# Where in a step two edge chunks share one TensorE product: a graph layer on one core

## The chip, the cores and the metric

The kernel runs on one core of a Trainium2 chip. A core has five engines with queues of their own: TensorE (matrix products; in the profile PE for the matmuls and PEld for the weight loads that go with them), VectorE (DVE), ScalarE (ACT), GpSimd (POOL) and SyncE (SP, which here only starts transfers). Sixteen DMA engines move data between HBM and the core's memory. The metric is the device time of one execution in microseconds.

## The reference

One layer of a graph network on 12,500 nodes of 128 numbers and 412,500 edges of 48 numbers, all float32. The edges are sorted by their destination node.

```python
h = jnp.maximum(_layernorm(x, axis=-1), 0.0)
agg = segment_sum(edge_attr_48, dst, num_segments=12500)      # 48 sums per node
u = graph_globals[0]                                           # the same for every node
hid = relu(concatenate([h, agg, u]) @ W1 + b1)                 # 240 -> 256
out = x + hid @ W2 + b2                                        # 256 -> 128
```

## The kernel before

**Chunks and steps.** 896 edges (128 partitions by T = 7) are a chunk. A step `s` takes CS = 8 chunks, 1.4 MB of edges, in two halves `h` of CH = 4 chunks; there are NS = 58 steps, the last one short. A chunk's edges go to a stretch of neighbouring nodes, and a one-hot matrix of W = 32 columns (`oh`, made by VectorE at L294) says which node of its window each edge belongs to.

**The sums of a step** (`aggregate`, from L314) are products of the one-hots (the weights) with the edges (the moving operand), added up in a PSUM tile `ps`. A single product takes one chunk and one value of t: 32 weight columns, 48 moving columns, and writes 32 of the 128 partitions; four of them, one for each chunk of a half, fill the partitions. A paired product takes two chunks at once: 64 weight columns and 96 moving columns. It gives four blocks of sums of which two are wanted; for the second chunk of a pair these lie in columns 48 to 95. One value of t in one half, a row in what follows, is thus four single products or two pairs. `twos[h]` is the number of rows of half `h` that are done in pairs; before the change they come first in the half (`t < twos`). Each product, being float32, leaves four records on TensorE: two weight loads and two matmuls.

**After the sums**, `keep_sums` (from L335, on ScalarE) copies `ps` to `sums`, with small copies of the odd chunks' other columns for the halves that have pairs. Two steps later (one in the last steps) `place` (TensorE, tile `pp`) moves the sums to their nodes and `add` (VectorE) adds them to the running table `aggT`.

**Between the sums** the layer itself runs in pieces, for blocks of 512 nodes: transposes of the normalised nodes (`turn`, tile `pt`), the first layer (`first_h`, `first_a`, tile `ph`), ReLU on ScalarE, the second layer (`second`, tile `po`), the result on VectorE and a store on GpSimd's queue. The order is written out by hand: a planner gives each piece a half-step `k` by a cost in us (`piece`), and the main loop emits for each step: `place`, the pieces of 2s, `add`, the pieces of 2s + 1, the sums, and ScalarE's copies.

**How many pairs.** The planner counts the products of the step, `n`, those since the last step's sums included, and reckons the time of TensorE, `us`, as 1.8 plus the pieces' costs. As long as `us` is below 0.08 us for each product, one more row is done in pairs, in the second and the first half by turns; a row adds 0.08 us to `us` and takes two from `n`. In the first steps `spare` products (a product of constants, L593 on, whose result nobody reads) are emitted at half-steps 1, 3, 5, 7 and 9.

**Loads.** SyncE issues the edges as 230 loads of two chunks, four to a step, three steps ahead. A load waits for the fifth load before it to land (`few`, at most 5 in flight) and for the TensorE product that was emitted last when the load was emitted. There are 18 buffers of two chunks.

At the end a flag tells whether the edges' order allowed all this; with these inputs the general path behind it (from L816 on) is not run.

Of the kernel before, what the change touches and what calls it, by code (L numbers as in the profile page):

```python
# [22 lines left out]
def kernel(  # L23
# [26 lines left out]
    T = 7  # L50
# [9 lines left out]
    NSF = NCH // CS  # L60
    TAIL = E - NCH * CE
    NS = NSF + 1
# [78 lines left out]
    with fast:  # L141
# [34 lines left out]
        def product(*a, **k):  # L176
            count[0] += 1
            last[:] = [nc.tensor.matmul(*a, **k).ins.name]  # L178
# [100 lines left out]
        def load(s, i):  # L279
            if s >= NS or s == NSF and i > 1:  # L280
                if s == NSF and i == 2:
                    edges[s].append(etail)
                return
            for c in (2 * i,):
                e = ep.tile([P, 2, T * DE], F32, name="e")
                few(load_edges(e, s * CS + c, 2))
                edges.setdefault(s, []).extend([e[:, 0], e[:, 1]])
                both.setdefault(s, []).append(e)

        def onehot(s):  # L290
            oh = ohp.tile([P, CH, T, 2, W], F32, name="oh")

            def compare(to, n, r):
                nc.vector.tensor_tensor(  # L294
                    to, iota[:, None, :W].to_broadcast([P, n, W]), r[:, :, None].to_broadcast([P, n, W]), OP.is_equal)

            def chunks(a, b):
                compare(oh[:, a // 2:b // 2].rearrange("p c t u w -> p (c t u) w"), (b - a) * T,
                        rel[:, (s * CS + a) // 2:(s * CS + b) // 2].rearrange("p c t u -> p (c t u)"))

            if s == NSF:
                chunks(0, CH)
                compare(oh[:, CH // 2, :TT, 0], TT, relt[:, :TT])
            elif s < 2:
                chunks(0, CH)
                chunks(CH, CS)
            else:
                chunks(0, CS)
            onehots[s] = oh
# [4 lines left out]
        def aggregate(s, h, twos):  # L314
            left = s == NSF and h
            if h == 0:
                banks_s[s] = ps_agg.tile([P, 512], F32, name="ps")[:, :4 * DE].rearrange("p (h f) -> p h f", h=2)
            ps, es, oh = banks_s[s], edges[s], onehots[s]
            n = TT if left else T
            for t in range(n):  # L320
                first, end = t == 0 and h == 0, t == n - 1
                if t < twos:
                    for q in range(0, CH, 2):
                        c = CH * h + q
                        product(ps[W * q:W * (q + 2), h], oh[:, c // 2, t], both[s][c // 2][:, :, t * DE:(t + 1) * DE],
                                start=first, stop=end, skip_group_check=True)
                    continue
                for q in range(1 if left else CH):
                    c = CH * h + q
                    o = DE * (q % 2) if twos else 0  # L330
                    product(
                        ps[W * q:W * (q + 1), h, o:o + DE], oh[:, c // 2, t, c % 2], es[c][:, t * DE:(t + 1) * DE],
                        start=first, stop=end, skip_group_check=True)

        def keep_sums(s, twos):  # L335
            ps = banks_s.pop(s)
            to = sums[s % NSB].rearrange("p h (u f) -> p h u f", u=2)[:, :, :, :DE]

            def keep_these(k, h, o):
                nc.scalar.copy(to[k, h], ps[k, h, None, o:o + DE].to_broadcast(  # L340
                    [k.stop - k.start, h.stop - h.start, 2, DE]))

            if s < NSF:
                keep_these(slice(0, P), slice(0, 2), 0)
            else:
                keep_these(slice(0, P), slice(0, 1), 0)
                keep_these(slice(0, W), slice(1, 2), 0)
            hs = [h for h in range(2) if twos[h]]
            for q in range(1, CH, 2) if hs else ():
                keep_these(slice(W * q, W * (q + 1)), slice(hs[0], hs[-1] + 1), DE)  # L350

        def place_columns(s):
            po = ohp.tile([P, 2, WP], F32, name="place")
            nc.vector.tensor_tensor(po, iota[:, None, :WP].to_broadcast([P, 2, WP]),  # L354
                                    pos[:, s, :, None].to_broadcast([P, 2, WP]), OP.is_equal)
            places[s] = po

        def place(s):
            banks_p[s] = pp = ps_p.tile([P, 512], F32, name="pp")
            po = places.pop(s)  # L360
            for h in range(2):
                k = W if s == NSF and h else P
                product(pp[:HI + DE, SECOND * h:SECOND * h + WP], sums[s % NSB][:k, h, :HI + DE], po[:k, h],
                                 start=(h == 0), stop=(h == 1), skip_group_check=True)

        def add(s):
            _, v = nc.values_load_multi_w_load_instructions(
                at_i[0:1, s:s + 1], engines=[DVE], min_val=low(s), max_val=high(s),
                skip_runtime_bounds_check_because="clamped to these on the chip")
            to = aggT[:, ds(v[0], WG)]  # L370
            nc.vector.tensor_tensor(to, to, banks_p.pop(s)[:HI + DE, :WG], OP.add)  # L371
# [186 lines left out]
        with tc.manual_schedule():  # L558
# [71 lines left out]
            def at(k, f, *a):  # L630
                todo.setdefault(max(0, k), []).append((f, a))


            def placed(s):
                return min(s + 2, max(LATE, s + 1))
# [48 lines left out]
            for j in range(NBL):  # L684
                k = where["turn", j]
# [13 lines left out]
            def apart(k, f, *a):  # L699
                while k - 1 in taken or k in taken or k + 1 in taken:  # L700
                    k -= 1
                taken.add(k)
                at(k, f, *a)
                return k
# [6 lines left out]
            at(6, middles, 1)  # L711
            at(10, check_dst, 0)
            at(12, check_dst, 1)
            for k in range(1, 10, 2):
                at(k, spare)
            for i in range(2, len(parts)):
                need = 2 * (parts[i][0] // CS - (4 if i == len(parts) - 1 else 0))
                k = apart(need - 4, middles, i)
                at(k + 2, check_dst, i)
                k = apart(k - 1, spread_dst, i, 1)  # L720
                k = apart(k - 1, spread_dst, i, 0)
# [5 lines left out]
            k = apart(2 * (NS - 6), verdict)  # L727
# [10 lines left out]
                at(where["turn", j], keep, j)  # L738
            assert placed(ready[x1]) < NS

            ALL, MORE, EACH_US = 1.8, 0.08, 0.08
            counted = count[0]
            for s in range(NS):
                now = [p for p in range(NS) if placed(p) == s]
                paced[:] = [s] * (s > 0)

                def next_load(i):
                    if s > 0:
                        load(s + AHEAD - 1, i)

                if s < LATE:
                    for p in now:
                        place(p)
                next_load(0)
                for f, a in todo.pop(2 * s, []):
                    f(*a)
                next_load(1)
                if s < LATE:
                    for p in now:
                        add(p)  # L760
                for f, a in todo.pop(2 * s + 1, []):
                    f(*a)
                next_load(2)
                if s >= LATE:
                    for p in now:
                        place(p)
                        add(p)


                us = ALL + work.get(2 * s, 0.0) + work.get(2 * s + 1, 0.0)  # L770
                n, twos = count[0] - counted + CS * T, [0, 0]
                for h in (1, 0) * T:
                    if us < EACH_US * n and s < NSF:
                        twos[h] += 1
                        us += MORE
                        n -= 2
                aggregate(s, 0, twos[0])
                aggregate(s, 1, twos[1])
                counted = count[0]
                next_load(3)  # L780
                keep_sums(s, twos)
                if s == 1:
                    place_columns(0)
                if s > 0:
                    place_columns(s)
                if s + EARLY < NS:
                    onehot(s + EARLY)
# [166 lines left out]
```

## Time and profile before

| | |
|---|---|
| time, median of 3 runs | 323.09 us (321.39 to 323.69) |
| the profiled execution | 322.37 us, its span 320.6 us |
| busy: TensorE, VectorE, ScalarE, GpSimd | 309.6, 232.4, 174.7, 77.2 us |
| bytes moved | 95.14 MB, 297 GB/s over the span |
| records on TensorE | 6171 matmuls, 6172 weight loads |
| first sums, last sums | 8.8 us, 305.3 us |

In a row of the timeline, the first number is the start in us from the span's start, the second how long the group lasts, then engine, source line, operation, written tile <- read tiles, the shape, and the number of records; in square brackets stands idle time before it and what ended it. Records of one line and the same tiles are merged, and a merged row shows the shape of its first record only. The shape 128*64 128x96 is a paired product, 128*32 128x48 a single one. Matmuls overlap and their ends are modelled, so a group's length overstates it: the distance from its start to the start of the next group is what it costs. In a row of the windows stand the stretch, its length, the busy time and number of records of each engine, the granted clock of TensorE, the share of the DMA engines and the rate in GB/s. A row of the waits names who waited, what ended it, the sum in us, the number of times and the longest.

### The profile page before, as it was taken

How to read it: one execution, taken by the hardware profiler on the slowest of the kernel's cores; microseconds unless marked ns; L12 is line 12 of the kernel's file. 1: busy time of each engine (PE TensorE's matmuls, PEld its weight loads, DVE VectorE, ACT ScalarE, POOL GpSimd, SP SyncE). 2: the span in 40 equal slices, each digit the busy share in tenths (PEclk: the TensorE clock that was granted, in tenths of full speed). 3: DMA queues.
4: the chain of work that ended last, by engine and by line, in shares of the span. 5: the costliest groups of instructions: out<-in, count | busy, mean ns of one | idle time of the engine just before them, and what ended most of it. 6: DMA issues, size and time to landing. Idle time of an engine off the chain costs nothing. (4 is left out here: it accounts for less than half of the span.)

```text
span 320.6 us, 14355 instructions
## 1 busy us (share of the span) xinstructions
PE 309.6 (97%) x6171; PEld 235.8 (74%) x6172; DVE 232.4 (72%) x530; ACT 174.7 (54%) x434; POOL 77.2 (24%) x87
## 2 busy tenths in 40 slices
PE   7899999999999999999999999999999999999992
PEld 3587767877787877776887886876787877887772
DVE  6786967785786866749966599769874899687221
ACT  2234795375564765555564486655552974565420
POOL 8221042022201444222224203113303034211000
PEclk9999999999999999999999999999999999999999
DMA  7999999999999999999999999999999999884102
GB/s 234 306 341 315 343 346 333 320 337 311 330 353 313 346 353 335 307 340 356 341 349 330 302 309 303 327 342 333 303 328 323 297 305 343 295 267 141 37 0 75
DMA packets 69716, 95.14 MB, mean 297 GB/s; under 512 B 5018, under 2 KB 64611, under 8 KB 69647
## 3 DMA queue, kind: packets, MB, share of 16 engines
q1 hardware_dynamic: 67439, 87.53, 83.5%
q0 software_dynamic: 2208, 6.63, 5.6%
q8 instruction: 50, 0.82, 1.0%
q14 instruction: 19, 0.16, 0.2%
HBM read 87.74 MB, written 6.40 MB: 294 GB/s over the span
## 5 line engine op out<-in xcount | busy, mean ns | idle before, releaser
L178 PEld LDWEIGHTS ps<-e,oh 128*32 128x32 f32 (+1 forms) x5056 | 108.4, 117 | 37.3 <-issue 8.4
L178 PE MATMUL ps<-e,oh 128*32 128x48 f32 (+1 forms) x5056 | 132.8, 221 | 0.7 <-issue 0.7
L294 DVE TENSOR_TENSOR oh<-iota,rel 128x1792 f32<-128x1792 f32 (+1 forms) x60 | 115.9, 1936 | 0.0
L340 ACT COPY sums<-ps 128x192 f32<-128x192 f32 (+1 forms) x173 | 53.6, 310 | 105.9 <-PE ps L178 103.3
L497 POOL DMA_DIRECT2D out_dram<-ot x25 | 13.9, 559 | 221.0 <-DVE ot L489 172.4
L371 DVE TENSOR_TENSOR aggT<-aggT,pp 112x246 f32 x58 | 23.7, 409 | 48.9 <-PE pp L178 41.3
L178 PE MATMUL po<-w,hid 128*128 128x128 f32 (+1 forms) x384 | 47.7, 276 | 1.3 <-ACTq L816 1.3
L411 POOL TENSOR_TENSOR xb<-xt,b_sb 128x512 f32<-128x512 f32 (+2 forms) x26 | 45.3, 1744 | 14.9 <-DMA xt<-in_x_dram 9.1
L178 PE MATMUL ph<-hT,w1h 128*128 128x512 f32 (+2 forms) x100 | 47.5, 578 | 0.3 <-ACT hT L432 0.3
L178 PEld LDWEIGHTS po<-w,hid 128*128 128x128 f32 (+1 forms) x384 | 44.9, 191 | 2.1 <-ACTq L816 1.4
L418 ACT ACTIVATE xn<-xt,sh,sc 128x128 f32<-128x128 f32 (+1 forms) x98 | 40.5, 482 | 1.1 <-DVE sh L405 0.6
L475 ACT ACTIVATE hid<-ph,bias 128x512 f32<-128x512 f32 (+2 forms) x49 | 30.3, 669 | 19.6 <-PE ph L178 18.4
L178 PE MATMUL pp<-place,sums 128*112 128x128 f32 x232 | 39.3, 292 | 0.0
L354 DVE TENSOR_TENSOR place<-iota,pos 128x256 f32<-128x256 f32 x58 | 34.8, 602 | 0.0
L178 PEld LDWEIGHTS pp<-place,sums 128*112 128x112 f32 x232 | 28.8, 176 | 5.1 <-issue 1.0
L178 PE MATMUL ph<-aggT,w1a 48*128 48x256 f32 (+1 forms) x192 | 28.4, 400 | 0.0
L432 ACT COPY hT<-pt 128x512 f32<-128x512 f32 (+2 forms) x26 | 26.6, 1022 | 0.8 <-PE pt L182 0.5
L489 DVE TENSOR_TENSOR ot<-po,xb 128x512 f32<-128x512 f32 (+2 forms) x25 | 16.6, 665 | 14.2 <-PE po L178 12.8
L178 PEld LDWEIGHTS ph<-aggT,w1a 48*128 48x128 f32 x192 | 17.3, 186 | 10.9 <-issue 7.8
L388 DVE BATCH_NORM_STATS2 st<-xt 128x6 f32<-128x128 f32 (+1 forms) x98 | 21.3, 278 | 1.9 <-DMA xt<-in_x_dram 1.9
L178 PEld LDWEIGHTS ph<-hT,w1h 128*128 128x128 f32 x100 | 16.2, 191 | 6.0 <-issue 3.3
L182 PE MATMUL pt<-ident,xn 128*128 128x128 f32 (+1 forms) x98 | 15.9, 282 | 0.2 <-DVE dev L239 0.2
(120 smaller groups left out, 143.3 us busy)
## 6 DMA issues: line engine op xcount, KB each, us to landing
e<-in_edge_attr_dram SPq DMA_DIRECT2D x230, 336.0 KB, 5.0
xt<-in_x_dram SPq DMA_DIRECT2D x23, 256.0 KB, 5.4
out_dram<-ot POOLq DMA_DIRECT2D x23, 256.0 KB, 5.0
di<-in_dst_dram SPq DMA_DIRECT2D x3, 448.0 KB, 6.9
xt<-in_x_dram SPq DMA_DIRECT2D x2, 128.0 KB, 4.5
out_dram<-ot SPq DMA_DIRECT2D x2, 128.0 KB, 2.8
di<-in_dst_dram SPq DMA_DIRECT2D x1, 154.0 KB
w1h<-in_L_gnn_W_dram POOLq DMA_DIRECT2D x1, 128.0 KB, 5.6
```

The costliest lines, as they stand in the source:

```text
L178: last[:] = [nc.tensor.matmul(*a, **k).ins.name]
L182: last[:] = [nc.tensor.transpose(*a, **k).ins.name]
L294: nc.vector.tensor_tensor(to, iota[:, None, :W].to_broadcast([P, n, W]), r[:, :, None].to_broadcast([P, n, W]), OP.is_equal)
L340: nc.scalar.copy(to[k, h], ps[k, h, None, o:o + DE].to_broadcast([k.stop - k.start, h.stop - h.start, 2, DE]))
L354: nc.vector.tensor_tensor(po, iota[:, None, :WP].to_broadcast([P, 2, WP]), pos[:, s, :, None].to_broadcast([P, 2, WP]), OP.is_equal)
L371: nc.vector.tensor_tensor(to, to, banks_p.pop(s)[:HI + DE, :WG], OP.add)
L388: nc.vector.bn_stats(st[:m, q, :], xs[j][:m, q, :])
L411: nc.gpsimd.tensor_tensor(xb[:m, :r], xs[j][:m, :r], b2_sb[:m, None, :].to_broadcast([m, r, D]), OP.add)
L418: nc.scalar.activation(xn[:m, q], xs[j][:m, q], AF.Relu, bias=shift[j][:m, q:q + 1], scale=scale[j][:m, q:q + 1])
L432: nc.scalar.copy(hT[:, :m * r].rearrange("d (p r) -> d r p", r=r), ht[j][:, :m * r].rearrange("d (r p) -> d r p", r=r))
L475: nc.scalar.activation(to, ph, AF.Relu, bias=bias[:, h:h + 1])
L489: nc.vector.tensor_tensor(ot[:m, :r], pos_o[j][:m, :r], xbs[j][:m, :r], OP.add)
```

## The change

Pairs are now put in the second half of a step alone, at its end: the last `twos` values of t. The time reckoned for TensorE starts at 1.75 instead of 1.8, and 0.15 more is asked before another row is paired. A step has 7 paired rows at most, and steps 54 on have none. The spare products at half-steps 5, 7 and 9 are gone. Worked through, 692 pairs become 576 and 1836 single products become 2068.

```diff
@@ aggregate
             for t in range(n):
                 first, end = t == 0 and h == 0, t == n - 1
-                if t < twos:
+                if t >= n - twos:
                     for q in range(0, CH, 2):
@@ spare products
-            for k in range(1, 10, 2):
+            for k in (1, 3):
                 at(k, spare)
@@ main loop
-            ALL, MORE, EACH_US = 1.8, 0.08, 0.08
+            ALL, TURN, MORE, EACH_US = 1.75, 0.15, 0.08, 0.08
...
                 us = ALL + work.get(2 * s, 0.0) + work.get(2 * s + 1, 0.0)
                 n, twos = count[0] - counted + CS * T, [0, 0]
-                for h in (1, 0) * T:
-                    if us < EACH_US * n and s < NSF:
-                        twos[h] += 1
-                        us += MORE
-                        n -= 2
+                while us + TURN < EACH_US * n and twos[1] < T and s < NS - 4:
+                    twos[1] += 1
+                    us += MORE
+                    n -= 2
```

## The prediction

> **What bounds the kernel now.** I read the page first, then TensorE's timeline step by step, then the waits of SyncE's queue, then the transfers.
>
> ```profile
> PE 309.6 (97%) x6171; PEld 235.8 (74%) x6172; DVE 232.4 (72%) x530; ACT 174.7 (54%) x434; POOL 77.2 (24%) x87
> PE   7899999999999999999999999999999999999992
> PEclk9999999999999999999999999999999999999999
> DMA  7999999999999999999999999999999999884102
> q8 instruction: 50, 0.82, 1.0%
> PE ps L178 <- issue: 0.7, 2, 0.5
> ```
>
> TensorE is busy from the first sums to the last, and in the list of waits its only entry inside the sums is 0.7 us of "issue". So TensorE's own work sets the time, and a microsecond taken out of it counts as long as nothing else is late. The transfers are busy in nearly every slice too, so they are the first candidate for "late". The third is the instruction stream itself: 50 packets of 0.82 MB together are 16 KB each, one for about every 250 of the 12,343 TensorE records (each product leaves four: two weight loads, two matmuls).
>
> What do the sums of one step cost? Both forms, and five steps with the start of whatever follows:
>
> ```profile
> L178 PE MATMUL ps<-e,oh 128*64 128x96 f32 x1384 | 81.9, 255 | 0.0
> L178 PE MATMUL ps<-e,oh 128*32 128x48 f32 x3672 | 62.2, 209 | 0.7 <-issue 0.7
> ...
> 15.94 2.53 PE L178 MATMUL ps<-e,oh 128*64 128x96 f32 x56
> 18.40 0.69 PE L178 MATMUL pp<-place,sums 128*112 128x128 f32 x4
> ...
> 114.55 2.00 PE L178 MATMUL ps<-e,oh 128*64 128x96 f32 x104
> 116.47 0.69 PE L178 MATMUL pp<-place,sums 128*112 128x128 f32 x4
> ...
> 206.58 2.16 PE L178 MATMUL ps<-e,oh 128*64 128x96 f32 x96
> 208.67 0.58 PE L178 MATMUL pp<-place,sums 128*112 128x128 f32 x3
> ...
> 150.06 2.32 PE L178 MATMUL ps<-e,oh 128*64 128x96 f32 x88
> 152.30 0.69 PE L178 MATMUL pp<-place,sums 128*112 128x128 f32 x4
> ...
> 301.09 1.77 PE L178 MATMUL ps<-e,oh 128*32 128x48 f32 x108
> 302.79 1.14 PE L178 MATMUL ph<-aggT,w1a 48*128 48x256 f32 x8
> ```
>
> A step has 14 rows (7 values of t in each half); a row is either four single products or two pairs. The merged rows carry the shape of their first product only, so the record count tells the mix: 104 records are 2 pair rows and 12 single rows, 96 are 4 and 10, 88 are 6 and 8, 108 are 1 and 13, and 56 are 14 pair rows. From start to start these take 1.92, 2.09, 2.24, 1.70 and 2.46 us.
>
> - From 2 to 6 pair rows the time grows by 0.32 us: **a pair row costs 0.08 us more than a single row**.
> - All pairs take 2.46. With 6 pair rows that would be 2.46 - 8 x 0.08 = 1.82, but it took 2.24. Such a step has three changes of form inside (pairs, singles | pairs, singles): **0.14 us for each turn**. The 108-record step, with one pair row and two turns, agrees: 2.46 - 13 x 0.08 + 2 x 0.14 = 1.70.
>
> **The change part by part.**
>
> *Turns and rows.* Working the two loops through with the counts of products, the old rule puts pairs in 346 rows with 161 turns (51 steps have three), the new one in 288 rows with 53 turns (one in each step that has pairs). Of that, steps 0 to 4 have 66 rows and 7 turns, then 35 and 5: 31 x 0.08 + 2 x 0.14 = 2.8 us. Steps 5 to 56 have 280 rows and 154 turns, then 253 and 48: 27 x 0.08 + 106 x 0.14 = 2.2 + 14.8 = **17.0 us** less work for TensorE. A new turn stands in the middle of the step, single to pair, as half of the old ones did, so I price it the same.
>
> *Three spare products.* One is worth what lies between its start and that of the sums:
>
> ```profile
> 18.93 1.02 PE L178 MATMUL ph<-iota,ones 128*128 128x512 f32 x2
> 19.89 2.74 PE L178 MATMUL ps<-e,oh 128*64 128x96 f32 x60
> ...
> 24.47 8.23 SPq L127 DMA_DIRECT2D e<-in_edge_attr_dram  x9
> e<-in_edge_attr_dram SPq DMA_DIRECT2D x230, 336.0 KB, 5.0
> 35.48 1.76 PE L178 MATMUL ps<-e,oh 128*64 128x96 f32 x54
> ```
>
> 0.96 us each, 2.9 in all, in steps 2, 3 and 4. But this work, and the 2.8 us of the same steps, lies over the arrival of the data. Counting four edge loads to a step, the seventh of the nine in the SyncE row, issued near 30 us, is the last of step 5. With the median of 5.0 us to landing it is there at 35.0, and step 5's sums start at 35.48 and need it 0.6 us later, in their second half. So of 5.7 us only about **0.5** can reach step 5; the rest becomes waiting for edges.
>
> *Loads for the rest of the run.* The loads have five in flight at most and are held to TensorE's pace.
>
> ```profile
> 137.90 8.51 SPq L127 DMA_DIRECT2D e<-in_edge_attr_dram  x9
> ...
> 286.27 2.32 SPq L127 DMA_DIRECT2D e<-in_edge_attr_dram  x3
> 304.66 0.80 PE L178 MATMUL ps<-e,oh 128*32 128x48 f32 x56
> ...
> SPq L127 <- DMA e<-in_edge_attr_dram: 58.0, 92, 2.0
> SPq L127 <- PE ps L178: 4.5, 9, 1.2
> ...
> SPq L127 <- PE ps L178: 17.5, 13, 2.6
> SPq L127 <- DMA e<-in_edge_attr_dram: 17.4, 32, 1.2
> ...
> 40.00:60.00 20.00, 19.74 (x438) 14.24 (x437) 13.45 (x32) 14.70 (x37) 5.68 (x6) 1.00 1.01 343
> 140.00:160.00 20.00, 19.52 (x432) 15.07 (x421) 15.82 (x38) 10.67 (x27) 3.62 (x5) 1.00 1.04 348
> 240.00:260.00 20.00, 20.00 (x430) 15.50 (x429) 14.35 (x38) 13.14 (x40) 4.83 (x5) 1.00 0.95 309
> ```
>
> The first pair of SyncE waits is from the window 40 to 190 us, the second from 190 to 290. In the first, loads wait for the landing of earlier loads; in the second as much for TensorE. The head start shows the same. At step 5 it is about nothing. The last load of step 27 (third of nine, near 139.7) lands near 144.7 for sums that start at 150.06: 5.4 us. The last of all is issued near 288.2 and lands near 293.2 for sums at 304.66: 11.5 us. So even on the old timetable the loads would let TensorE be some 11 us earlier at the end, and more where the pace held them back (348 GB/s were moved in one window, 309 in a late one). On the way it is tighter: by step 27 TensorE would gain about 22 x 0.31 (two turns a step and some rows) + 0.5 = 7.3, against 5.4 + 0.6 of head start. I take **2.5 us** of waiting for edges after step 5; the ends are 0 (the loads speed up with TensorE's pace) and 10 (they don't).
>
> *The instruction stream.* 116 pairs fewer are 116 products more, less three spares: 452 more records.
>
> ```profile
> 58.08 1.11 PE L178 MATMUL ps<-e,oh 128*32 128x48 f32 x32 [0.26 <-issue]
> 141.69 0.49 PE L178 MATMUL ps<-e,oh 128*32 128x48 f32 x26 [0.48 <-issue]
> ...
> 57.90:141.60 83.70, 83.13 (x1773) 63.93 (x1773) 60.92 (x131) 48.37 (x115) 22.76 (x21) 1.00 1.00 330
> ```
>
> These are the two "issue" waits, each inside a run of singles, with no data to wait for. Between them lie 3546 TensorE records: 14 blocks of 253, the size of a packet with some semaphore instructions in it. I read them as two late packets. The sums run from 8.8 to 305.3 us, so 12,343 / 253 = 48.8 blocks last 296 / 48.8 = 6.1 us each; 12,795 / 253 = 50.6 in 284 would last 5.6. If every boundary comes 0.5 us sooner, the two late ones are late by some 0.9 each, and a few more, now just in time, are late by a few tenths: **3 us more**, an estimate; the ends are 0 and 25 (all 50 late by 0.5).
>
> On this the Trainium skill, "Runtime: NRT & Kernel Launch", section Instruction fetch mechanics, speaks: instructions come in 16 KiB blocks of 256, fetched ahead, and crossing a block is "mostly hidden" because dispatch is slower than the fill. The block size agrees with the rows above, the two stalls do not bear out the hiding; by the rule the term would be 0 and the time 307.7.
>
> *The rest.* ScalarE's small copies after a step now take one half instead of two, and none in steps 54 to 56; ScalarE is at 54% and the result is placed a step later, so nothing. VectorE goes from 72% to about 75% of a shorter span; nothing unless a one-hot comes late. The weights of the layer, the final products and the last store are unchanged. The pairs now stand after the singles, so nothing new waits ahead of the next step's work except the loads of the second half, which are needed as before.
>
> **Sum.** 17.0 + 0.5 - 2.5 - 3.0 = 12.0. The profiled span is 320.6 and that execution took 322.37, so 310.4; the median of the three timed runs, 323.09, is 0.7 above, which gives 311.1. I predict 310.7. A change under about 1%, 3 us, could not be told from none.
>
> **The rivals.**
>
> 1. *All of TensorE's gain.* The loads follow and the packets stay hidden: 17.5 less, 305.6. For it: the head start of 11.5 us. Against: windows at a DMA share of 1.0 already, and two late packets.
> 2. *The transfers take over.* Singles let TensorE ask for edges faster than 340 GB/s. If the first half of the run stays on its old timetable, the gain there is no more than the head start, and a few us come in the second half: 4 to 7 less than the median, about 317. For it: the 58.0 us of waiting for landings. Against: the loads get ahead of TensorE all the same.
> 3. *The instruction stream takes over (slower).* If TensorE is really fed at one block in 6.1 us, cheaper rows give nothing and 452 more records cost 1.8 blocks: 11 us, 334. It decides once most blocks arrive later than they are used up, 5.6 us. Against: only two such waits in some 48 blocks.
> 4. *A cold clock.* The spare products may be there to keep TensorE at speed.
>
> ```profile
> 1.68 2.07 PE L178 MATMUL ph<-iota,ones 128*128 128x512 f32 x2 [1.68 <-POOL iota L565]
> 5.06 3.78 PE L178 MATMUL ph<-iota,ones 128*128 128x512 f32 x4
> 13.20 0.73 PE L182 MATMUL pt<-ident,df 128*128 128x128 f32 x4 [1.16 <-ACT sums L340]
> ```
>
> Early spares take about twice as long as the one at 18.93 (four in 3.78 against two in 1.02), though the granted clock of the page stands at 9 tenths or more throughout. If the waits for edges in steps 2 to 4, 1 to 1.5 us each, bring that state back, some 8 us of work there last twice as long and about 4 us of it are not covered: 314.7. Against: after 1.16 us of idleness at 13.20 four transposes run at full speed. The Trainium skill, "TensorE: Matmul & The Clock Gate", Part 1, has the clock halve after an idle window of about 3.4 us; no wait that I foresee is so long.
> 5. *It does nothing.* If a turn were a wait for the next chunk's edges and not a cost of the change of form, it would stay: only 27 x 0.08, 2 us, eaten by the packets, 322. Against: the same 0.14 at 150 us, where the edges are 5 us ahead.
>
> **How the numbers follow.** Forecast (307 to 314.5) 0.62; all of the gain 0.08; transfers 0.17; cold clock 0.03; nothing 0.05; slower 0.05. The range 305 to 318.5 takes in the first four but for their edges and leaves out 1 to 2 in 10. Faster by over 1% means below 319.9: 0.62 + 0.08 + 0.17 + 0.03 less 0.03 of the slow end of the transfers, 0.87; within 1% 0.07; slower 0.06.
>
> **What the changed profile would show.** A step with 12 pairs takes 1.96 from its first sum to the next operation, one without pairs 1.34. The entry "issue" inside the sums grows from 0.7 to some 3 us. Waits for edges appear on TensorE in steps 1 to 5 and here and there to step 30. Windows from 40 to 280 move near 340 GB/s. I am wrong if the turns stay at the old price in the new place, if "issue" reaches 10 us, or if TensorE waits for edges in most steps.

## The result and the profile after

The changed kernel takes 312.40 us (median of 4 runs, 310.81 to 314.13) beside 322.24 for the kernel before: a ratio of 0.9694, 95% interval 0.9624 to 0.9765. Timed again with five rounds it took 310.15 us beside 321.83: 0.9637 (0.9601 to 0.9673). Here and below a median is that of all executions, while ratios and intervals leave out slow ones, those over 1.5% above the fastest of the same kernel. The forecast was 310.7, 12.0 us less. The profiled execution of the changed kernel took 310.81, its span is 309.1: 11.5 us less than the span before.

First the page and the waits of the changed kernel, where TensorE's own load was to shrink and "issue" to grow:

```profile
PE 291.4 (94%) x6397; PEld 227.5 (74%) x6398; DVE 231.8 (75%) x530; ACT 164.1 (53%) x426; POOL 78.5 (25%) x87
PEclk9997999999999999999999999999999999999999
q8 instruction: 51, 0.84, 1.1%
...
PE ps L178 <- issue: 4.6, 9, 1.0
PEld ps L178 <- DMA e<-in_edge_attr_dram: 4.6, 8, 0.8
PE ps L178 <- DMA e<-in_edge_attr_dram: 2.5, 5, 0.6
```

226 matmuls and as many weight loads more, the 452 records of the forecast. TensorE is busy 18 us less, and inside the sums it waits more: 4.6 us of issue instead of 0.7, and for edges, which it did not wait for before.

The price of the sums, from the timeline of TensorE (start of the sums, start of what follows), for steps with 4, 8, 12 and no pairs:

```profile
111.06 1.71 PE L178 MATMUL ps<-e,oh 128*32 128x48 f32 x104
112.70 0.69 PE L178 MATMUL pp<-place,sums 128*112 128x128 f32 x4
...
199.22 1.87 PE L178 MATMUL ps<-e,oh 128*32 128x48 f32 x96
201.02 0.69 PE L178 MATMUL pp<-place,sums 128*112 128x128 f32 x4
...
150.61 2.03 PE L178 MATMUL ps<-e,oh 128*32 128x48 f32 x88
152.57 0.69 PE L178 MATMUL pp<-place,sums 128*112 128x128 f32 x4
...
290.04 1.40 PE L178 MATMUL ps<-e,oh 128*32 128x48 f32 x112
291.37 1.14 PE L178 MATMUL ph<-aggT,w1a 48*128 48x256 f32 x8
```

1.64, 1.80, 1.96 and 1.33 us, where the first three mixes took 1.92, 2.09 and 2.24 before: 0.28 us less with the same number of pairs, two turns. That is the gain, read off three steps.

Where the run as a whole gained, the starts of the sums of step 5 and of the last step show:

```profile
31.61 1.37 PE L178 MATMUL ps<-e,oh 128*64 128x96 f32 x26 [0.54 <-DMA e<-in_edge_attr_dram]
...
35.75 2.03 PE L178 MATMUL ps<-e,oh 128*32 128x48 f32 x88
...
293.24 0.80 PE L178 MATMUL ps<-e,oh 128*32 128x48 f32 x56
```

Step 5 starts at 35.75 instead of 35.48: the first five steps gained nothing, and step 4 can be seen waiting for edges ahead of its pairs. From step 5 to the last step it is 257.49 us instead of 269.18, 11.69 less. What follows takes 15.9 us in both. So of 17.0 us of work saved, some 5.3 were lost again on the way, to packets, edges or both; the experiments are about that.

SyncE's waits between 190 and 290 us, the two rows that were equal before:

```profile
SPq L127 <- DMA e<-in_edge_attr_dram: 41.4, 64, 2.0
...
SPq L127 <- PE ps L178: 0.8, 3, 0.3
```

The pace of TensorE holds the loads back no longer (0.8 us instead of 17.5); they wait for earlier loads to the end of the run.

### The profile page after: what moved, and what is told of

Read it like the earlier page. It is cut to its first block, busy times and chain, and to the rows that moved or that the text cites. A ratio compares the mean times of both kernels' runs of the same rounds, so it can differ in the third digit from the quotient of the medians.

```text
span 309.1 us, 14799 instructions
## 1 busy us (share of the span) xinstructions
PE 291.4 (94%) x6397; PEld 227.5 (74%) x6398; DVE 231.8 (75%) x530; ACT 164.1 (53%) x426; POOL 78.5 (25%) x87
## 5 line engine op out<-in xcount | busy, mean ns | idle before, releaser
L178 PE MATMUL ps<-e,oh 128*32 128x48 f32 (+1 forms) x5288 | 117.6, 218 | 7.2 <-issue 4.6
L178 PEld LDWEIGHTS ps<-e,oh 128*32 128x32 f32 (+1 forms) x5288 | 100.7, 116 | 31.4 <-issue 10.2
L340 ACT COPY sums<-ps 128x192 f32<-128x192 f32 (+1 forms) x165 | 43.1, 262 | 97.5 <-PE ps L178 94.9
L411 POOL TENSOR_TENSOR xb<-xt,b_sb 128x512 f32<-128x512 f32 (+2 forms) x26 | 46.5, 1792 | 15.3 <-DMA xt<-in_x_dram 9.8
L182 PE MATMUL pt<-ident,xn 128*128 128x128 f32 (+1 forms) x98 | 15.9, 282 | 0.0
```

The source lines that it names most:

```text
L182: last[:] = [nc.tensor.transpose(*a, **k).ins.name]
L411: nc.gpsimd.tensor_tensor(xb[:m, :r], xs[j][:m, :r], b2_sb[:m, None, :].to_broadcast([m, r, D]), OP.add)
```

## The experiments

The theory: turns are what the change saves, and late instruction packets and late edges, both through the traffic of the edges, take part of it back. The rivals: the counts of pairs make the gain; the spare products matter; the packets are late whatever the traffic.

**Place alone, counts alone.** The first keeps the old counts and spares and gathers the pairs at the end of the step; the second has the change's counts, split over the halves as before.

```diff
-                if t < twos:
+                if t >= n - twos:
...
+                both_h = sum(twos)
+                twos = [max(0, both_h - T), min(T, both_h)]
                 aggregate(s, 0, twos[0])
```

> The old counts of pairs (346 rows) and all five spare products, but the pairs gathered at the end of the step, second half first, so that one turn is left in a step (55 in all instead of 161). If a turn costs 0.14 us, steps 5 to 56 lose 102 x 0.14 = 14.3 us of TensorE work; with as many records as before in less time I expect some 1.5 us more of late packets and about 0.5 of waits for edges: 310 us (308 to 313), as fast as the change or a little faster. Rival (the counts make the gain, the place does not): 320 us or more.

```diff
-                if t >= n - twos:
+                if t < twos:
...
+                twos = [twos[1] // 2, twos[1] - twos[1] // 2]
                 aggregate(s, 0, twos[0])
```

> The change's counts (288 rows, two spares, no pairs in the last four steps), but split over both halves and first in each, as before: 159 turns. By the turns, TensorE has 10 x 0.14 + 27 x 0.08 = 3.6 us less work after step 5 than the kernel before, of which more late packets (more records) take back 2 or so: 320.5 us (318.5 to 322.5). Rival (fewer pairs make the gain): about 312.

Place alone: 312.19 us (308.47 to 317.71), ratio 0.9646 (0.9556 to 0.9736). Counts alone: 318.40, ratio 0.9899 (0.9845 to 0.9952). Step 5 and the last step in the two timelines, place alone first, and the issue waits of each:

```profile
35.18 2.03 PE L178 MATMUL ps<-e,oh 128*32 128x48 f32 x88
...
294.59 0.59 PE L178 MATMUL ps<-e,oh 128*32 128x48 f32 x36
...
PE ps L178 <- issue: 3.6, 6, 1.1
```

```profile
35.76 1.43 PE L178 MATMUL ps<-e,oh 128*64 128x96 f32 x46
...
301.19 0.80 PE L178 MATMUL ps<-e,oh 128*32 128x48 f32 x56
...
PE ps L178 <- issue: 0.3, 2, 0.2
```

Place alone saves 269.18 - 259.41 = 9.8 us on this stretch, of 14.3 priced; counts alone 269.18 - 265.43 = 3.75, of 3.6 priced. So the place of the pairs makes the gain. The two miss in opposite ways. Place alone has not one record more than the kernel before and yet has late packets; counts alone has the 452 more and none. So more records alone do not make packets late, and my 2 us of packets for counts alone were wrong. The mean pace does not tell the two apart either: from the first sums to the last, 253 records take 5.9 us in place alone and 5.8 in counts alone.

**Half the edges.** Only the first of every two loads is made, the sums take its edges twice.

```diff
+            if i % 2:
+                e = both[s][-1]
+                edges[s].extend([e[:, 0], e[:, 1]])
+                both[s].append(e)
+                return
             for c in (2 * i,):
```

> The kernel before with only the first of every two edge loads of a step; the sums take those edges twice, so the output is not the layer's. TensorE's products are the same, the traffic is about half. If TensorE's own work sets the time of the kernel before, it hardly moves: 320 us (318.5 to 321.5), with no issue wait inside the sums if late packets come from the traffic.

> The same cut of the edge loads in the changed kernel. With neither edges nor, if they are late through traffic, instruction packets in the way, the whole of the priced work should show: 17.0 after step 5 and most of 5.7 in steps 0 to 4, so 20 to 23 us under the kernel before with half the loads: 297 to 300 us. If the packets are late by themselves (4.6 us of issue stays), 302 to 304. If the turns were mis-priced, the difference to the kernel before with half the loads says by how much.

The kernel before hardly moves: 320.53 us, ratio 0.9965 (0.9943 to 0.9986). The changed one comes to 300.71, 0.9354 (0.9320 to 0.9389), 19.8 us under it. Step 5 and the last step, before with half the loads, then the change with half the loads and its waits:

```profile
34.33 2.32 PE L178 MATMUL ps<-e,oh 128*64 128x96 f32 x88
36.57 0.69 PE L178 MATMUL pp<-place,sums 128*112 128x128 f32 x4
...
302.23 0.80 PE L178 MATMUL ps<-e,oh 128*32 128x48 f32 x56
```

```profile
14.35 2.11 PE L178 MATMUL ps<-e,oh 128*32 128x48 f32 x84
16.39 0.69 PE L178 MATMUL pp<-place,sums 128*112 128x128 f32 x4
...
26.54 3.02 PE L178 MATMUL ps<-e,oh 128*32 128x48 f32 x84
29.49 1.20 PE L178 MATMUL pp<-place,sums 128*112 128x128 f32 x4
...
33.03 2.03 PE L178 MATMUL ps<-e,oh 128*32 128x48 f32 x88
34.99 0.69 PE L178 MATMUL pp<-place,sums 128*112 128x128 f32 x4
...
284.00 0.80 PE L178 MATMUL ps<-e,oh 128*32 128x48 f32 x56
...
PE ps L178 <- issue: 0.2, 1, 0.2
...
PE pt L182 <- DVE dev L239: 1.7, 1, 1.7
```

267.90 and 250.97: **16.9 us between step 5 and the last, where 17.0 were priced.** The issue waits are gone with the traffic. Step 5, with 12 pairs, costs 2.24 and 1.96 us here (start to start), as the same mix does with all the loads: a turn is not a wait for edges. Against these, the kernel before loses 269.18 - 267.90 = 1.3 us to the traffic on this stretch, the changed one 257.49 - 250.97 = 6.5. The difference, 5.2, is what the forecast had as 2.5 + 3.0.

What these losses are can be read off matmul by matmul, since a kernel runs the same matmuls with all the loads and with half. From step 5 to the last step, the changed kernel loses 5.9 of its 6.5 us in nine jumps that stand where a new block of 256 TensorE instructions begins (the records with a few semaphore instructions), 0.3 at the one wait for edges, at 160.8 us, and 0.4 little by little. The kernel before loses 1.2 of 1.3 us at its two issue waits. So of the 5.2 us, packets are some 4.6 and edges 0.3.

That the issue waits are waits for packets also shows in the packets of queue q8. The eight of over 0.2 us in the sums of the change lie 256 instructions or a multiple apart, to within one, and end 1.2 to 1.5 us after a 16 KB packet has landed. A block's packet is fetched, for the most part, while the block before it runs. After 36 us its fetch starts a median of 2.2 us behind the start of that block in the change and in place alone, 1.9 in the kernel before, 1.7 in counts alone, and 0.9 in the change with half the loads; the fetch itself takes 1.0 to 1.1 us in all of them. So the traffic makes packets late by holding up the start of their fetch. Why it holds it up more in place alone than in counts alone is not shown.

In the first five steps the change gains only 1.3 us (34.33 to 33.03) even here, of 5.7 of removed work. In part VectorE is late there instead, as the 1.7 us wait for `dev` shows. In part it is the clock: in this execution the granted clock is at 0.50 from 27.5 to 31.0 us, and the sums of step 4 cost 2.95 us (from 26.54) where those of step 1, as many records, cost 2.04 (from 14.35). This was the slowest of five executions, 302.79 us; the others took 300.60 to 300.96.

**No pairs at all**, with all the loads and with half.

```diff
-                while us + TURN < EACH_US * n and twos[1] < T and s < NS - 4:
+                while False:
```

> The change with no pairs at all: 288 x 0.08 + 53 x 0.14 = 30 us less TensorE work than the change, 576 products (2304 records, 9 packets) more. If only TensorE's work counted: 283. If the edges are the floor that the change has already reached, 311 to 313, TensorE idling some 20 us for edges and packets. If the instruction stream is the harder limit (59.7 packets at 5 us or more each), 316 or more, and the issue waits inside the sums are above 15 us.

> No pairs, and only the first of every two edge loads (the sums take those edges twice). TensorE has 30 us less work than in the change with half the loads (300.7). If the packets of no_pairs were late through the edge traffic, most of the 30 us shows: 272 to 285, with issue waits below 8 us. If the instruction stream cannot follow singles whatever the traffic, 295 or more with issue waits above 20 us.

329.42 us (324.45 to 330.32, with no ratio on record; the kernel before beside it 320.28 to 323.11), slower than the kernel before in every execution although TensorE has, by the forecast's prices, 47 us less of work than there: the 17 of the change and, for its 288 pair rows at 0.08 and 53 turns at 0.14, 30 more. With half the loads 295.84, ratio 0.9136 (0.9039 to 0.9232). The issue waits, all loads first:

```profile
PE 276.2 (84%) x7549; PEld 213.7 (65%) x7550; DVE 233.3 (71%) x530; ACT 136.7 (42%) x320; POOL 75.5 (23%) x87
PEclk9896999999999999899999999799799997999998
...
PE ps L178 <- issue: 36.1, 33, 3.6
```

```profile
PE ps L178 <- issue: 17.6, 21, 2.7
```

Here the third rival decides: 15,099 records are 59.7 blocks of 253, and TensorE gets through them in about 303 us, 5.1 us each (4.5 with half the loads), against 5.6 in the change and 6.1 before. Traffic alone does not make the packets late, since 17.6 us of waits stay with half of it, and 295.84 lies in the second case of the expectation, not in the 272 to 285 of the first; only 5 of the 30 us of removed work show (the medians are from two chips; from step 5 to the last step it is 6.8). The waits are not all of the loss with all the loads: the granted clock is at 0.50 for 23.9 us in all (6.8 with half), five of the six falls coming in such a wait or within 1.3 us of its end, and the same products keep TensorE busy for 276.2 us instead of 262.9. So a pair is worth its 0.08 us where it keeps TensorE from running ahead of its instructions. Where between the change and no pairs that turns was not measured.

**Loads and spares.** Seven loads in flight instead of five, and the spare products put back; then, on one chip and with five rounds, the change again beside spares back, spares back with seven loads, and place alone with seven loads.

```diff
-        FLIGHT = 5
+        FLIGHT = 7
...
-            for k in (1, 3):
+            for k in range(1, 10, 2):
```

> The change with seven loads in flight instead of five. If the window of five limits the rate (5 x 344 KB in 5.1 us is 337 GB/s, what was moved), the edges come sooner, waits for edges vanish and the time is 308 to 310. If the rate is the memory's own, each load takes about 7 us instead of 5.1 and the time stays at 312; if deeper queues hold up the instruction packets, the issue waits grow and it is 313 to 316.

> The change with the spare products at half-steps 5, 7 and 9 put back. If they only cover waits for edges, the time stays within 1 us of the change's 312.4, and the granted clock, which fell to 0.91 between 20 and 40 us in the change's profile, is 1.00 throughout. If the spares cost their 0.96 us each, 315. If the half-speed stretch of the change cost it time to the end, 311 or less, with step 5 starting before 35.5 us.

> The changed kernel itself, beside the next three on one chip: 312 us again.

> The change with its three spare products put back, against the change on the same chip. If the half-speed stretch behind the missing spares costs time to the end, 1.5 to 2.5 us less than the change (310); if the spares only fill waits, the same within 0.7 us.

> The change with the spares back and seven loads in flight. If the half-speed stretch and the window of five cost about 1.5 us each and separately, 309; if both only move the same waits for edges, 310 to 311; packets delayed by deeper queues show as more than 6 us of issue in the sums.

> The old counts of pairs and all spares, pairs gathered at the end, seven loads in flight. 58 more pair rows than the change are 4.6 us more of TensorE work, 452 records fewer should take back 2 to 3 us of late packets: 310 to 313. If the packets are nearly free, 313 to 315; if they cost more than the rows, under 309.5.

| | us | ratio to before | 95% interval |
|---|---|---|---|
| seven loads | 310.96 | 0.9665 | 0.9628 to 0.9702 |
| spares back | 310.29 | 0.9640 | 0.9580 to 0.9699 |
| the change again | 310.15 | 0.9637 | 0.9601 to 0.9673 |
| spares back again | 311.39 | 0.9695 | 0.9664 to 0.9726 |
| spares back, seven loads | 310.21 | 0.9667 | 0.9618 to 0.9716 |
| place alone, seven loads | 313.94 | 0.9750 | 0.9708 to 0.9792 |

With seven loads in flight the loads take longer, and the time is the same:

```profile
e<-in_edge_attr_dram SPq DMA_DIRECT2D x230, 336.0 KB, 5.8
...
PE ps L178 <- issue: 5.5, 10, 1.1
```

5.8 us to landing instead of 5.1, between the two cases of the expectation, and the time does not change: the window of five is not what holds the run. The spares are worth nothing that these runs can tell, either way: side by side they are 1.2 us apart in favour of the change, with touching intervals. Place alone with seven loads, where edges cannot be late (0.3 us of waits), is 3.8 us slower than the change on the same chip, and its issue wait, 5.0 us, is the same as there. Of its 58 more pair rows, 31 stand in the first five steps, and step 5 starts at 34.36 us, as in the change (34.37); the 27 others and four more turns are priced at 2.7 us, and from step 5 to the last step it takes 3.2 longer. None of the variants beats the change beyond its interval.

## Why the prediction was right

**Turns and rows, 17.0 us: right.** Single steps show 1.64, 1.80, 1.96 and 1.33 us (1.96 and 1.34 were foretold for two of them), and half the loads show 16.9 for the sum. With the place undone 3.75 us of the gain are left.

**Spares and the first steps, 0.5 us: not there in the profile** (0.3 later). In the second profile of the change step 5 starts at 34.37, 1.1 earlier, so this term is uncertain by about a microsecond. The reason given, that the edges arrive no sooner, is half of it: with half the edges, VectorE and a stretch of halved clock hold the same steps, and 1.3 of the 5.7 us is all that profile shows.

**Edges 2.5 and packets 3.0: the sum 5.5 was right, 5.2 measured; the split was not, and that the sum fits is luck.** After 36 us TensorE's list of waits in the sums has one entry:

```profile
PE ps L178 <- issue: 4.3, 8, 1.0
```

The comparison with half the loads puts some 4.6 us on packets and 0.3 on edges. The step that failed is the price of the edges, 2.2 us too high. The head start was read rightly, and the loads used the time that TensorE's pace had cost them, which is the lower end that the forecast named; of the waits "here and there to step 30" there is one. The packets were 1.6 too low. Their reason was right, that blocks are used up sooner than before, but nine blocks came late by 0.2 to 1.2 us where I had two by 0.9 and a few by some tenths. In the second profile of the change the same stretch takes 258.25 us instead of 257.49, so these sizes hold to about a microsecond.

**The total.** 17.0 + 0.5 - 2.5 - 3.0 = 12.0 stands against 16.9 - 0.3 - 5.2 = 11.4 in the profile, and 9.8 and 11.7 in the two sets of medians.

**The rivals.** "All of the gain" is what half the loads give, from step 5 on, so the traffic is what stood against it. "The transfers take over" did not come: the loads are busy to the end, but TensorE waits for them only at the start and once for 0.3 us. "The instruction stream takes over" was rated 0.05 and is the mechanism nearest to it: without pairs it makes the kernel slower than before. "It does nothing" is out, since a turn costs the same with half the loads. "A cold clock" did come, in the first profile:

```profile
25.72 2.50 PE L178 MATMUL ps<-e,oh 128*64 128x96 f32 x26 [0.58 <-DMA e<-in_edge_attr_dram]
...
25.80:29.00 3.20, 3.20 (x30) 2.98 (x31) 2.22 (x15) 0.70 (x3) 1.27 (x1) 0.50 0.89 278
```

Step 3's pairs run at half the granted clock. In the second profile the clock stays at 1.00 over the same steps and step 5 starts 1.4 us sooner, but that execution took 310.40 us, this one 310.81. None of the seven profiles with all five spare products has such a stretch, and of the seven with two, five have one between 13 and 35 us. So the spares seem to keep the clock up, as this rival supposed. What that is worth at the end lies below what the medians can tell; at step 5 it is the 1.4 us, not the 4 it was priced at.

The rule of the Trainium skill, "Runtime: NRT & Kernel Launch", section Instruction fetch mechanics, that crossing a block of 256 instructions is "mostly hidden", would have given 307.7. In the change most crossings are hidden, but nine waits in the sums of some 50 blocks add up to 4.6 us; without pairs, with 33 waits and 36.1 us, the rule does not hold.

## What to carry to other kernels

Price a change of product shape on TensorE by itself: put all products of one form side by side, and compare steps with different mixes to get the price of a turn and of a row. When TensorE is made faster, ask what feeds it: here, without pairs, it waited at 33 of some 60 block boundaries, so products that do more per instruction can be worth their extra time. A run with less traffic and the same products shows how much of a gain the traffic takes back, and laying the two traces side by side, matmul by matmul, shows where.

## What the runs showed of the hardware

TensorE's clock halved without a long wait. In the 3.4 us before it fell at 25.7 us, TensorE was busy for 2.28 and no single idle time was above 0.6:

```profile
22.20:25.60 3.40, 2.28 (x68) 1.75 (x66) 2.60 (x6) 1.66 (x6) 1.08 (x2) 1.00 1.05 370
```

The Trainium skill, "TensorE: Matmul & The Clock Gate", Part 1, asks for an idle window of about 3.4 us; the stretch at half speed has about that length here, but the window before it was far from idle. In the second profile a similar stretch did not lower the clock. In all profiles there are eleven such falls between the first 10 us and the last products, and in the 3.41 us before each TensorE was busy for 0.7 to 2.2 us, so none needed a wholly idle window. One with 1.6 us passed without a fall (without pairs, ending at 54.8 us), so what decides it stays open.
